# Layer 2's transposed input, written and read with a step of four floats, in a four-layer graph network kernel

## The chip, the cores and the metric

The kernel runs on one core of a Trainium2 chip, in one launch. The metric is the device time of one execution in microseconds (us), lower is better; every time shown is from the chip. The engines of a core, as the profile names them: PE is TensorE's products, PEld its weight loads (a product has a *stationary* operand, which is loaded first, and a *moving* one, which streams past it), DVE is VectorE, ACT is ScalarE, POOL is GpSimd, SP is SyncE, which here issues transfers. SBUF is the memory on the core that all engines work in, PSUM the one that TensorE writes its results to; both have 128 partitions.

## The reference

Thirty-two inputs of 512 nodes with 128 features pass through four graph layers that share one 0/1 adjacency matrix. After each layer its input is added and each node is normalised over its features. Cut to what matters:

```
x = layernorm(x + L0(x))      # attention over neighbours
x = layernorm(x + L1(x))      # attention over neighbours, elu
x = layernorm(x + L2(x))      # below
x = layernorm(x + L3(x))      # adj @ x + x, weights, each row divided by its norm

def L2(input, adj, W, e, bias):
    h0 = einsum('bnf,fg->bng', input, W[0])
    h1 = einsum('bnf,fg->bng', input, W[1])
    A = softmax(where(adj > 0, vals, NEG), axis=1)
    M = eye(N)
    return einsum('ij,bjg->big', A * M, h0) + einsum('ij,bjg->big', A * (1 - M), h1) + bias
```

All arrays are float32: `x` is (32, 512, 128), `adj` (512, 512), `W` (2, 128, 128). Layer 2 weighs a node by `W[0]` and its neighbours by `W[1]`. With the `e` of these inputs, which is all ones, every row of `A` is 1/degree over the row's neighbours, and the kernel computes layer 2 as (input W0 + (neighbour sum of input) W1) / degree.

## The kernel before

A node matrix of one input is a tile of 128 partitions by 512 columns: four *chunks* of 128 nodes, each 128 nodes by 128 features, side by side (`NCH` is 4, `P` is 128). TensorE contracts over partitions, so a product "nodes by features times weights" needs its left operand with the features on partitions. Where a layer needs its input that way, there is a transposed tile `xt`, features by 512 nodes.

The work of one input is cut into some 90 *units*, small functions that each issue one or a few instructions: `pt2` is layer 2's transposes, `xt2` the copy of their result, `py2` the neighbour sum, and so on. A unit is registered with the names of the tiles that it uses. The table `PLAN` gives each unit and input a place in one global order of some 3,260 places, or -1 if it isn't used for that input. Once, while the program is built, the order is sorted and the units are issued one after the other; each engine then works through its own instructions in that order, and semaphores make it wait for what others produce. Units of several inputs are interleaved, so that all engines have work. A unit that is registered and has no row in `PLAN` issues nothing. Buffers come from stocks of fixed size (`kind`), are taken when a tile is first used, and are given back after its last use.

Layer 2, for each of the 32 inputs:

- `pt2` (lines 170 to 174): TensorE transposes the four chunks of `x2`, with the identity as moving operand and the chunk as stationary one, into a PSUM bank `pt2` of 512 columns; chunk c goes to columns c*128 to c*128+127. For `pt0` (four inputs) and `pt1` (five inputs) the same line writes each chunk through `swapped`, as four runs of 32 columns that lie 128 apart. All other inputs get their transposed tiles of layers 0 and 1 another way: for layer 0 a reordered load and VectorE, for layer 1 VectorE's transpose (`tr1`), a transfer to DRAM (`tw1`) and four transfers back (`tb1`), which SP issues.
- `xt2` (line 178): ScalarE copies the whole bank to SBUF.
- `py2` and `y2` (lines 303 and 307): the neighbour sums, features by nodes, and their copy.
- `po2` (lines 317 and 318): for each chunk of nodes, the chunk of `y2` as stationary operand with `W[1]`, and onto it the chunk of `xt2` as stationary operand with `W[0]`. These are layer 2's last products.
- `o2s`, `v2p`, then the normalisation: the division by the degree on ScalarE (line 397), the addition of input and bias on GpSimd (line 401), statistics on VectorE (lines 360 and 362), and so on to layer 3.

Other lines that come up: 230 transposes a single column that is broadcast to 128 (the stationary operand reads one address 128 times), 217 is the product of the attention, 515 the sixteen transposes at the start that warm TensorE up, 591 transposes in bf16.

Of the kernel before, what the change touches and what calls it, by code (L numbers as in the profile page):

```python
# [10 lines left out]
F32 = mybir.dt.float32  # L11
# [7 lines left out]
P = 128  # L19
Q = 32  # L20
# [6 lines left out]
def kernel(  # L27
# [18 lines left out]
    nc = tc.nc  # L46
    B, N, F = x.shape
    NCH = N // P
# [9 lines left out]
    dram = fast.enter_context(tc.tile_pool(name="dram", bufs=1, space=bass.MemoryType.DRAM))  # L58

    def chunks(t):  # L60
        return t.rearrange("p (c f) -> p c f", c=NCH)
# [40 lines left out]
    w20, w21, w3_s = (const.tile([F, F], F32, name=n) for n in ("w20", "w21", "w3_s"))  # L102
# [12 lines left out]
    def kind(name, count, names, make):  # L115
        STOCK[name] = (count, make)
        for n in names.split():
            KIND[n] = name

    def plain(shape, dtype=F32):  # L120
        return lambda name: store.tile(list(shape), dtype, name=name)
# [13 lines left out]
    kind("rn", 12, "rn0 rn1 rn2 rn3", plain([P, 2, NCH]))  # L135
    kind("rs", 12, "rs0a rs0b rs1a rs1b", plain([P, 2]))
    kind("ss", 6, "ss", plain([P, NCH]))
    kind("dt", 4, "dt1", lambda name: dram.tile([P, N], F32, name=name))
    kind("rb", 4, "rb0 rb1", plain([P, N]))
    kind("rt", 4, "rt0 rt1", plain([P, Q]))  # L140
    kind("rd", 4, "rd0 rd1", lambda name: dram.tile([N], F32, name=name))
# [1 line left out]
    def unit(name, *tiles):  # L143
        def register(fn):
            UNITS[name] = (fn, tiles)
        return register

    def swapped(t):
        return t.rearrange("p (a c i) -> p c a i", a=NCH, c=NCH)

    def pair(t, half):
        return t[:, 2 * half : 2 * half + 2]

    @unit("ld", "x0")
    def _(b, x0):
        nc.sync.dma_start(chunks(x0), x[b].rearrange("(c p) f -> p c f", p=P))
# [7 lines left out]
    @unit("tr0", "sw0", "xt0")  # L164
    def _(b, sw, xt):
        nc.vector.transpose(swapped(xt), sw)

    for k in range(3):

        @unit(f"pt{k}", f"x{k}", f"pt{k}")  # L170
        def _(b, xk, p, k=k):
            for c in range(NCH):
                dst = swapped(p)[:, c] if k < 2 else p[:, c * P : (c + 1) * P]
                nc.tensor.transpose(dst, xk[:, c * P : (c + 1) * P], ident)  # L174

        @unit(f"xt{k}", f"pt{k}", f"xt{k}")
        def _(b, p, xt):
            nc.scalar.copy(xt, p)

    @unit("tr1", "x1", "tr1")  # L180
    def _(b, x1, tr):
        nc.vector.transpose(tr.rearrange("p (f c i) -> p c f i", f=NCH, c=NCH), x1)

    @unit("tw1", "tr1", "dt1")
    def _(b, tr, dt):
        nc.sync.dma_start(dt, tr)

    @unit("tb1", "dt1", "xt1")
    def _(b, dt, xt):
        for f in range(4):  # L190
            src = bass.AP(tensor=dt.tensor, offset=dt.offset + f * P, ap=[[N, Q], [Q * N, P // Q], [1, P]])
            nc.sync.dma_start(xt[f * Q : (f + 1) * Q, :].rearrange("p (a n) -> p a n", n=P), src)

    for k in range(2):
        for half, s in enumerate("ab"):
# [31 lines left out]
        @unit(f"pr{k}", f"pr{k}")  # L227
        def _(b, p, k=k):
            for c in range(NCH):
                nc.tensor.transpose(swapped(p)[:, c], exps[:, 2 * b + k, 0, c : c + 1].to_broadcast([P, P]), ident)  # L230
# [82 lines left out]
    @unit("po2", "y2", "xt2", "po2")  # L313
    def _(b, y, xt, p):
        for c in range(NCH):
            cols = slice(c * P, (c + 1) * P)
            nc.tensor.matmul(p[:, cols], y[:, cols], w21, start=True, stop=False)  # L317
            nc.tensor.matmul(p[:, cols], xt[:, cols], w20, start=False, stop=True)  # L318

    @unit("po3", "y3", "po3")  # L320
    def _(b, y, p):
# [89 lines left out]
    for c in range(NCH):  # L411
        cols = slice(c * P, (c + 1) * P)
# [224 lines left out]
    def _(b, p):  # L637
# [336 lines left out]
    order = sorted([(t, -1, name) for name, t in STARTS.items()]  # L974
                   + [(t, b, name) for name, ts in PLAN.items() for b, t in enumerate(ts) if t >= 0])
    users = Counter((b, t) for _, b, name in order for t in UNITS[name][1])
    home = {}
    for name, (count, make) in STOCK.items():
        FREE[name] = deque(make(f"{name}_{i}") for i in range(count))

    with tc.manual_schedule():
        first()
        for _, b, name in order:
            fn, tiles = UNITS[name]
            for t in tiles:
                if (b, t) not in home:
                    home[b, t] = FREE[KIND[t]].popleft()
            fn(b, *[home[b, t] for t in tiles])
            for t in tiles:
                users[b, t] -= 1  # L990
                if not users[b, t]:
                    FREE[KIND[t]].append(home.pop((b, t)))
# [317 lines left out]
```

## Time and profile before

| | |
|---|---|
| time, median of 3 runs | 554.61 us (552.77 to 554.64) |
| the profiled execution | 553.77 us |
| its span, first to last instruction | 552.1 us |
| mean granted TensorE clock | 0.992 |
| PE busy | 530.7 us, 96%, 4116 instructions |
| PEld busy | 501.5 us, 91%, 4116 |
| DVE busy | 499.1 us, 90%, 1913 |
| ACT busy | 472.1 us, 86%, 1868 |
| POOL busy | 405.7 us, 73%, 673 |
| line 318, products of `xt2` with `W[0]` | 256 records, 49.5 us busy, 275 ns mean |
| line 317, products of `y2` with `W[1]` | 256 records, 49.5 us busy, 275 ns mean |
| line 174, transposes from `x1` and `x2` | 148 records, 21.7 us busy, 273 ns mean |
| line 178, copies of the transposed tiles | 41 instructions, 591 ns median |

Durations on PE overlap: a product is shown from its start until its result is written, while the next has begun. Busy time of a group is the time in which at least one of its instructions runs. A product of two float32 operands shows up as two pairs of a weight load and a product, so the 128 calls of line 318 (32 inputs by 4 chunks) are 256 records; a transpose is one pair. Weight loads run beside products.

### The profile page before, as it was taken

To read this page: it belongs to the slowest core of one execution; us is meant where nothing else is said; L and a number is where in the kernel's file an instruction comes from. 1 tells how busy PE (TensorE), PEld (TensorE's weight loads), DVE (VectorE), ACT (ScalarE), POOL (GpSimd) and SP (SyncE) were. 2 spreads that over 40 slices of the span, in tenths; PEclk is the share of its full clock that TensorE was granted. 3 is DMA by queue.
4 is the path that set the end of the run, shared out by engine and by line. 5 is a ranking of instruction groups with operands and counts; after the bars stand their busy time and mean duration, and the time that the engine had idled before them with its cause. 6 is when DMAs were issued, how large, how long until landed. Compare 5 with 4: busy or idle time off the path is not lost.

```text
span 552.1 us, 13985 instructions
## 1 busy us (share of the span) xinstructions
PE 530.7 (96%) x4116; PEld 501.5 (91%) x4116; DVE 499.1 (90%) x1913; ACT 472.1 (86%) x1868; POOL 405.7 (73%) x673
## 2 busy tenths in 40 slices
PE   7999999999999999999999999999999999999971
PEld 7899999999999999999999999999999999998850
DVE  2799999999999999999999999999999986787475
ACT  3768678988898789888989898898899899989994
POOL 4223795677948868688698776778688878889973
PEclk9999999999999999999999999999999999999996
DMA  7333344536357454446453544545203211000013
GB/s 211 67 83 92 78 117 111 123 93 174 97 136 173 103 139 87 131 112 161 115 136 97 150 106 128 156 99 121 90 20 117 78 39 40 20 21 2 21 57 100
DMA packets 124449, 55.22 MB, mean 100 GB/s; under 512 B 65744, under 2 KB 113488, under 8 KB 124368
## 3 DMA queue, kind: packets, MB, share of 16 engines
q1 hardware_dynamic: 123792, 53.94, 38.4%
q8 instruction: 34, 0.56, 0.4%
q10 hardware_dynamic: 576, 0.33, 0.3%
q14 instruction: 47, 0.39, 0.2%
HBM read 38.67 MB, written 15.58 MB: 98 GB/s over the span
## 4 chain that ended last, share of the span: by engine, by line
PE 76%; DVE 11%; ACT 8%; POOL 2%; issue 1%; DMA 1%; ACTq 0%; DVEq 0%
PE ps L217 37%; PE ps L303 15%; PE ps L200 9%; DVE al L255 4%; PE ps L317 4%; PE ps L318 4%; PE ps L324 4%; PE ps L174 2%; DVE st L360 2%; ACT sq L334 1%; ACT sq L383 1%; DMA acols<-in_L_gnn_a_dst_dram 1%; ACT sq L307 1%; PE ps L230 1%; ACT sq L397 1%
## 5 line engine op out<-in xcount | busy, mean ns | idle before, releaser
L217 PE MATMUL ps<-hp,al 128*128 128x129 f32 x2048 | 244.7, 275 | 0.7 <-POOL off L579 0.5
L217 PEld LDWEIGHTS ps<-hp,al 128*128 128x128 f32 x2048 | 237.4, 191 | 2.7 <-POOL off L579 0.7
L255 DVE SCALAR_TENSOR_TENSOR al<-rb,exps,mp 128x512 f32<-128x512 f32 x216 | 145.6, 735 | 1.2 <-DMA rb<-rd 1.2
L360 DVE BATCH_NORM_STATS2 st<-sq 128x6 f32<-128x128 f32 x508 | 108.2, 274 | 11.1 <-POOL sq L401 7.7
L390 POOL TENSOR_SCALAR sq<-sq,rn 128x128 f32<-128x128 f32 x252 | 113.0, 465 | 3.5
L383 ACT ACTIVATE sq<-sq,rn 128x128 f32<-128x128 f32 x256 | 106.2, 503 | 5.8 <-POOL rn L378 5.6
L210 ACT ACTIVATE hp<-ps,exps 128x128 f32<-128x128 f32 x256 | 89.6, 431 | 0.3
L296 POOL TENSOR_TENSOR xr<-sq,xr 128x512 fp32r<-128x512 f32 x64 | 83.2, 1304 | 7.3 <-DVE st L360 3.8
L200 PE MATMUL ps<-we,sq 128*128 128x131 f32 x512 | 71.2, 277 | 0.1
L303 PE MATMUL ps<-off,xr 128*128 128x512 f32 x256 | 67.6, 406 | 0.0
L303 PE MATMUL ps<-a3t,xr 128*128 128x512 f32 x256 | 67.3, 404 | 0.2 <-POOL xr L296 0.2
L200 PEld LDWEIGHTS ps<-we,sq 128*128 128x128 f32 x512 | 65.4, 192 | 2.0 <-issue 0.5
L286 POOL TENSOR_TENSOR sq<-sq,x 128x512 f32<-128x512 f32 x32 | 41.8, 1307 | 24.0 <-DVE sq L272 13.4
L378 POOL TENSOR_TENSOR rn<-mv,rn 128x4 f32<-128x4 f32 x127 | 28.4, 229 | 41.6 <-ACT rn L374 25.3
L286 POOL TENSOR_TENSOR sq<-sq,sq 128x512 f32<-128x512 f32 x32 | 43.4, 1356 | 17.8 <-DVE sq L280 12.4
L303 PEld LDWEIGHTS ps<-a3t,xr 128*128 128x128 f32 x256 | 46.3, 189 | 10.1 <-POOL xr L296 0.6
L303 PEld LDWEIGHTS ps<-off,xr 128*128 128x128 f32 x256 | 45.9, 189 | 9.1 <-DVE sq L262 0.2
L317 PE MATMUL ps<-w,sq 128*128 128x128 f32 x256 | 49.5, 275 | 0.0
L318 PE MATMUL ps<-w,sq 128*128 128x128 f32 x256 | 49.5, 275 | 0.0
L362 DVE BATCH_NORM_AGGREGATE mv<-st 128x2 f32<-128x9 f32 x508 | 48.7, 157 | 0.0
L401 POOL TENSOR_TENSOR sq<-sq,sq 128x512 f32<-128x512 f32 x32 | 41.1, 1286 | 9.8 <-ACT sq L397 6.9
L268 ACT ACTIVATE sq<-ps,rs 128x128 f32<-128x128 f32 x128 | 39.7, 376 | 8.4 <-DVE rs L221 8.3
(116 smaller groups left out, 918.4 us busy)
## 6 DMA issues: line engine op xcount, KB each, us to landing
rb<-rd SPq DMA_DIRECT2D x54, 256.0 KB, 3.8
x<-in_x_dram SPq DMA_DIRECT2D x32, 256.0 KB, 4.0
out_dram<-sq SPq DMA_DIRECT2D x31, 256.0 KB, 2.3
sw<-in_x_dram SPq DMA_DIRECT2D x112, 64.0 KB, 3.6
dt<-sq SPq DMA_DIRECT2D x27, 256.0 KB, 2.4
sq<-dt SPq DMA_DIRECT2D x108, 64.0 KB, 2.2
rd<-rt SPq DMA_DIRECT2D x54, 2.0 KB, 1.7
an<-in_adj_dram SPq DMA_DIRECT2D x3, 256.0 KB, 4.9
```

The lines of the kernel that those rows point to most:

```text
L200: nc.tensor.matmul(twos(p)[:, c, :FE], xt[:, (2 * half + c) * P : (2 * half + c + 1) * P], ATT[k], start=True, stop=True)
L210: nc.scalar.activation(h[:, 2 * half + c, :F], twos(p)[:, c, :F], AF.Identity, bias=pc if k else 0.0, scale=pc)
L217: nc.tensor.matmul(twos(p)[:, c, : F + 1], al[:, j, rows], h[:, j, :], start=(j == 0), stop=(j == NCH - 1))
L255: nc.vector.scalar_tensor_tensor(al[:, j, :], r, exps[:, 2 * b + k, 2, j : j + 1], mask[:, j, :], op0=ALU.max, op1=ALU.mult)
L286: nc.gpsimd.tensor_add(o, o, xk)
L296: nc.gpsimd.tensor_sub(xl, xk, xh.bitcast(F32))
L303: nc.tensor.matmul(p, part[:, j * P : (j + 1) * P], mat[:, j, :], start=(i + j == 0), stop=(i + j == NCH))
L317: nc.tensor.matmul(p[:, cols], y[:, cols], w21, start=True, stop=False)
L318: nc.tensor.matmul(p[:, cols], xt[:, cols], w20, start=False, stop=True)
L360: nc.vector.bn_stats(st[:, c, :6], o[:, c * P : (c + 1) * P])
L383: nc.scalar.activation(xo[:, c * P : (c + 1) * P], o[:, c * P : (c + 1) * P], AF.Identity, bias=rn[:, 1, c : c + 1], scale=rn[:, 0, c : c ...
L390: nc.gpsimd.tensor_scalar(xo[:, c * P : (c + 1) * P], o[:, c * P : (c + 1) * P], rn[:, 0, c : c + 1], rn[:, 1, c : c + 1], op0=ALU.mult, o ...
```

## The change

A new view `mixed` of a 512-column tile takes column n*4+c as column n of chunk c: the columns of a chunk lie four floats (16 bytes) apart, and the four chunks are interleaved. `pt2` writes its transposes through it, `xt2` copies all 512 columns as before, and `po2` reads its stationary operand through it, so that what is computed stays the same. In the same edit the three units `tr1`, `tw1`, `tb1` become a loop that registers `tr2`, `tw2`, `tb2` as well, and the DRAM tile's name `dt2` is added. `PLAN` is untouched, and it has no row for the new units.

```diff
-    kind("dt", 4, "dt1", lambda name: dram.tile([P, N], F32, name=name))
+    kind("dt", 4, "dt1 dt2", lambda name: dram.tile([P, N], F32, name=name))
...
+
+    def mixed(t):
+        return t.rearrange("p (n c) -> p c n", c=NCH)
...
         @unit(f"pt{k}", f"x{k}", f"pt{k}")
         def _(b, xk, p, k=k):
             for c in range(NCH):
-                dst = swapped(p)[:, c] if k < 2 else p[:, c * P : (c + 1) * P]
+                dst = swapped(p)[:, c] if k < 2 else mixed(p)[:, c]
                 nc.tensor.transpose(dst, xk[:, c * P : (c + 1) * P], ident)
...
-    @unit("tr1", "x1", "tr1")
-    def _(b, x1, tr):
-        nc.vector.transpose(tr.rearrange("p (f c i) -> p c f i", f=NCH, c=NCH), x1)
...
+    for k in (1, 2):
+
+        @unit(f"tr{k}", f"x{k}", f"tr{k}")
+        def _(b, xk, tr, k=k):
+            nc.vector.transpose(tr.rearrange("p (f c i) -> p c f i", f=NCH, c=NCH), xk)
...
@@ -315,7 +320,7 @@
         for c in range(NCH):
             cols = slice(c * P, (c + 1) * P)
             nc.tensor.matmul(p[:, cols], y[:, cols], w21, start=True, stop=False)
-            nc.tensor.matmul(p[:, cols], xt[:, cols], w20, start=False, stop=True)
+            nc.tensor.matmul(p[:, cols], mixed(xt)[:, c], w20, start=False, stop=True)
```

More of the change, by code (lines that the diff above doesn't have):

```diff
@@ L178, in _ @@
             nc.scalar.copy(xt, p)
-    @unit("tr1", "x1", "tr1")
-    def _(b, x1, tr):
-        nc.vector.transpose(tr.rearrange("p (f c i) -> p c f i", f=NCH, c=NCH), x1)
[L184 to L192, printed above, removed]
+    for k in (1, 2):
+        @unit(f"tr{k}", f"x{k}", f"tr{k}")
+        def _(b, xk, tr, k=k):
+            nc.vector.transpose(tr.rearrange("p (f c i) -> p c f i", f=NCH, c=NCH), xk)
+        @unit(f"tw{k}", f"tr{k}", f"dt{k}")
+        def _(b, tr, dt):
+            nc.sync.dma_start(dt, tr)
+        @unit(f"tb{k}", f"dt{k}", f"xt{k}")
+        def _(b, dt, xt):
+            for f in range(4):
+                src = bass.AP(tensor=dt.tensor, offset=dt.offset + f * P, ap=[[N, Q], [Q * N, P // Q], [1, P]])
+                nc.sync.dma_start(xt[f * Q : (f + 1) * Q, :].rearrange("p (a n) -> p a n", n=P), src)
     for k in range(2):
```

## The prediction

> **What bounds the kernel now.** I read the busy table by stretches first, to see which engine is full where.
>
> ```profile
> core 0: us, PE busy (x) PEld busy (x) DVE busy (x) ACT busy (x) POOL busy (x), PEclk, DMA share, GB/s
> ...
> 72.00:200.00 128.00, 127.69 (x1013) 121.70 (x1013) 126.19 (x468) 112.70 (x432) 96.70 (x148) 1.00 0.51 125
> 200.00:350.00 150.00, 150.00 (x1192) 143.40 (x1191) 149.34 (x577) 135.26 (x549) 117.20 (x196) 1.00 0.50 126
> 350.00:480.00 130.00, 130.00 (x1011) 123.26 (x1009) 118.44 (x462) 116.90 (x471) 104.24 (x167) 1.00 0.28 76
> 480.00:524.40 44.40, 44.30 (x299) 39.92 (x298) 30.22 (x141) 41.27 (x167) 41.62 (x62) 1.00 0.04 13
> 524.40:552.10 27.70, 11.39 (x60) 8.25 (x58) 17.15 (x83) 19.55 (x100) 15.73 (x33) 0.84 0.26 78
> ```
>
> Each entry is busy us and, in brackets, instructions. From 72 to 524.4 us, where every product of `po2` lies, TensorE is idle 0.31 + 0 + 0 + 0.10 = 0.41 us. VectorE is nearly as full up to 350 us, so the plan holds two engines at their limit there, but what is added to TensorE has no gap to go into. Second, the chain of waits, which says the same in one line:
>
> ```profile
> PE 76%; DVE 11%; ACT 8%; POOL 2%; issue 1%; DMA 1%; ACTq 0%; DVEq 0%
> ```
>
> Third, the two changed lines, 318 (weight load and product) and 174 (transposes), with the two groups that I use as measures:
>
> ```profile
> L318 PEld LDWEIGHTS ps<-w,sq x256: 191/192/192, 72.7 to 524.2; 128*128 128x128 f32 x128
> L318 PE MATMUL ps<-w,sq x256: 275/275/275, 72.8 to 524.3; 128*128 128x128 f32 x128
> ...
> L174 PEld LDWEIGHTS ps<-ident,sq x148: 137/141/147, 32.5 to 517.7; 128*128 128x128 f32 x148
> L174 PE MATMUL ps<-ident,sq x148: 270/273/299, 32.6 to 517.8; 128*128 128x128 f32 x148
> ...
> L230 PEld LDWEIGHTS ps<-ident,exps x40: 133/137/139, 12.7 to 480.5; 128*128 128x128 f32 x40
> ...
> L515 PE MATMUL ps<-ident x16: 418/418/473, 1.4 to 4.7; 128*128 128x128 f32 x16
> ```
>
> Durations (min/median/max, ns) of neighbours overlap, so what an instruction costs TensorE is the step from one start to the next. The timeline gives it for one `po2`:
>
> ```profile
> 256.37 0.30 PEld L318 LDWEIGHTS ps<-w,sq 128*128 128x128 f32 x2
> 256.48 0.39 PE L318 MATMUL ps<-w,sq 128*128 128x128 f32 x2
> 256.59 0.30 PEld L317 LDWEIGHTS ps<-w,sq 128*128 128x128 f32 x2
> 256.70 0.39 PE L317 MATMUL ps<-w,sq 128*128 128x128 f32 x2
> ...
> 259.90 0.60 PE L174 MATMUL ps<-ident,sq 128*128 128x128 f32 x4
> 260.34 1.96 PE L217 MATMUL ps<-hp,al 128*128 128x129 f32 x16
> ```
>
> A call in the program is two records here (x2): 256.48 to 256.70 is 0.22 us for two, so one load with its product takes a slot of **0.111 us**. Four transposes take 260.34 - 259.90 = 0.44 us, 0.110 each. A load begins as the product ahead of it begins, 0.11 us before its own product; there is one load per product, and no slot without one.
>
> **The change, part by part.** Registered but never issued: `tr2`, `tw2`, `tb2` (PLAN has no row for them) and the name `dt2`; the stock of `dt` stays 4. No instruction is added, removed or moved, no wait and no DMA. The copy `xt2` (line 178, 0.591 us) still reads 512 neighbours. Two access patterns are left.
>
> *The write of `pt2`.* Line 174 has 148 + 16 = 164 transposes: 4 in each of 4 `pt0`, 5 `pt1` and 32 `pt2`, so 128 of `pt2` now write every fourth float. The nearest row is the same line: the 36 of `pt0` and `pt1` already write four runs of 32 with gaps between, and min and max over the 148 that read `sq` (20 of `pt1` among them) are 270 and 299 ns. Nothing there speaks for a price, and nothing for a gain: low end 0. High end: a slot twice as long. The slowest steady 128-column group is line 515's warm-up, 16 starts from 1.4 to 4.7 us, 3.3 / 15 = 0.22, against 0.110: at most 0.11 x 128 = 14.1 us. I take 0, by the nearest row, and keep 14.1.
>
> *The load of `xt2` in `po2`.* Line 318 has 256 loads, each of 128 floats per partition, so far neighbours in 512 bytes, now 16 bytes apart over 2,048. No row of the trace loads with such a step. Low end: line 230's loads read one address 128 times and take 137 ns, line 174's read 128 neighbours and take 141, so pattern has cost 4 ns at most, and even the most local one starts its products no sooner; that excludes a gain of note. In proportion to the bytes spanned, (2048 - 512) / 512 x 4 = 12 ns a load would be added, 3.1 us in all if none of it is hidden. High end: the load's fetch takes twice its slot, 0.22 in place of 0.111 as in line 515, 0.109 us more. 256 x 0.109 = 27.9 us. The ends lie far apart. I take the **high end**, because of what the load rows vary with: 98 ns for the 128x128 of line 591 in bf16, 141 for a transposing load in f32, 192 for a load of a product in f32. The same 128 columns differ by 94 ns by how they are fetched, so fetching, and not a fixed time, fills a good part of line 318's slot, and line 230's repeated address is no test of separate fetches.
>
> [...]
>
> *What hides any of it.* The product ahead of a load covers 0.111 us, and that cover is in use in full, as loads already follow one another at that step. Of idle time, 0.41 us shows; gaps below the 0.16 us by which records overlap (0.275 - 0.111) don't. At 0.111 for 3,604 records and (259.90 - 257.96) / 8 = 0.24 for the 512 of line 303, TensorE's work is 400 + 123 = 523 us of its 530.7 busy, and some 4 to 5 us of the rest are slow starts before 25 us. I let 3 us be taken up. What is late next: `o2s` on ScalarE reads each `po2`, then the sum on GpSimd and layer 2's normalisation; these have slack once TensorE sets a slower beat (ScalarE 135.26 of 150, GpSimd 117.20). VectorE, at 149.34 of 150, gains idle time. After 524.4 us no changed instruction runs, and that tail shifts as a whole.
>
> **Sum.** 27.9 + 0 - 3 = 24.9 us. The profiled execution took 553.77 us, 1.7 around its span of 552.1. 553.77 + 24.9 = 578.7; the median of the three runs, 554.61, is 0.84 higher, so **579.5 us**.
>
> **Rivals.**
>
> *Both patterns pay.* 579.5 + 14.1, about 594. For: both steps leave every neighbour behind. Against: the gapped writes of `pt0` and `pt1`, at the same duration.
>
> *Nothing is slower (the other side).* The place is line 318's slot. Its load shows 192 ns but has 0.111 us of TensorE to itself, so 81 ns overlap anyway; as long as the strided fetch ends within that slot the next product starts as before, and the time is 554.6. It decides from a fetch of 0.111 us on: below, the stride is free; each ns above costs 0.256 us. For: lines 230 and 174 differ by 4 ns. Against: no idle time anywhere if the slot is passed. The 12 ns by bytes spanned would give 554.6 + 3.1 = 557.7 less what is taken up, 555 to 558.
>
> *The write alone pays.* 554.6 + 14.1 = 568.7, some 568 after small gaps. For: in `pt2` the transposes follow one another at 0.110 too. Against: as above.
>
> *Faster.* Only a load below today's could do it, and 137 against 141 ns brought none.
>
> **How the numbers follow.** Load alone 0.30 (own range 574 to 584), both 0.26, write alone 0.13, a load price between 12 and 109 ns 0.05 (560 to 572), nothing 0.17, the small price by bytes 0.06, faster 0.03. The likeliest gives 579.5. A measurement of this kernel tells 0.5% (2.8 us) from no change: slower holds 0.30 + 0.26 + 0.13 + 0.05 and half of the 0.06, 0.77; same 0.17 + 0.03 = 0.20; faster 0.03. The range runs from 553, below the case of nothing, to 594, which leaves out the upper half of both (0.13) and the 0.03.
>
> **What would show it.** In the changed profile: line 318's loads longer than 192 ns by tens, and 0.43 us for two records of line 318 in the timeline where 0.22 stand now, while line 317 keeps 0.22; line 174's four transposes still 0.44 (0.88 if the write pays); line 178 still 0.591. TensorE stays full up to the last `po2`, which starts some 25 us later, and the tail after it keeps its 27.7 us. The forecast is wrong if line 318's step stays at 0.111, if line 174 takes over 0.11 each, or if the load slows and idle time elsewhere pays for it.

## The result, and the profile after

The changed kernel takes 581.02 us (median of 4 runs, 580.16 to 582.2) beside 554.43 us (4 runs, 552.77 to 554.64): 1.05 times as long, 95% interval 1.0466 to 1.0534. The profiled execution has a span of 580.0 us where 552.1 us stood, 27.9 us more. Lines have moved down: 174, 178, 230, 303, 317, 318 and 397 of before are 177, 181, 235, 308, 322, 323 and 402 now.

First the table by stretches, with its last bound at the end of the changed products (busy us, instructions in brackets, in the columns shown above for before):

```profile
200.00:350.00 150.00, 150.00 (x1115) 143.47 (x1115) 143.40 (x539) 128.52 (x514) 113.24 (x185) 1.00 0.51 123
350.00:500.00 150.00, 150.00 (x1112) 143.74 (x1111) 131.89 (x512) 128.03 (x511) 111.69 (x180) 1.00 0.26 73
500.00:551.20 51.20, 51.20 (x305) 46.72 (x304) 30.21 (x141) 44.10 (x175) 44.38 (x65) 1.00 0.06 17
551.20:580.00 28.80, 12.95 (x60) 9.58 (x59) 17.29 (x83) 18.84 (x96) 14.36 (x32) 0.74 0.23 67
```

TensorE (first busy entry) is full as before, yet from 200 to 350 us it gets through 1,115 products where it did 1,192. VectorE (third) falls from 149.34 to 143.40 us there: it has more idle time. The chain of waits names TensorE for 92% of the span where it named it for 76%:

```profile
PE 92%; DMA 3%; ACT 2%; DVE 1%; SPq 0%; issue 0%; POOL 0%; DVEq 0%
```

Next the changed lines, by source line (min/median/max ns, first and last start us):

```profile
L323 PEld LDWEIGHTS ps<-w,sq x256: 309/320/332, 70.9 to 551.0; 128*128 128x128 f32 x128
L323 PE MATMUL ps<-w,sq x256: 392/396/398, 71.0 to 551.1; 128*128 128x128 f32 x128
...
L177 PEld LDWEIGHTS ps<-ident,sq x148: 138/141/264, 30.7 to 543.7; 128*128 128x128 f32 x148
L177 PE MATMUL ps<-ident,sq x148: 271/273/299, 30.9 to 543.9; 128*128 128x128 f32 x148
```

The loads of `xt2` went from 192 to 320 ns, 128 ns more for 128 columns, and the products beside them from 275 to 396. The transposes that write with the step stand at 273 ns as before. The timeline of the same `po2` as shown before gives the slots:

```profile
263.64 0.38 PE L322 MATMUL ps<-w,sq 128*128 128x128 f32 x2
263.86 0.63 PE L323 MATMUL ps<-w,sq 128*128 128x128 f32 x2
264.32 0.39 PE L322 MATMUL ps<-w,sq 128*128 128x128 f32 x2
264.54 0.63 PE L323 MATMUL ps<-w,sq 128*128 128x128 f32 x2
...
268.25 0.60 PE L177 MATMUL ps<-ident,sq 128*128 128x128 f32 x4
268.68 1.96 PE L222 MATMUL ps<-hp,al 128*128 128x129 f32 x16
```

From 263.64 to 263.86 line 322's two records take 0.22 us as before; from 263.86 to 264.32 line 323's two take 0.46, so 0.23 each in place of 0.111. The lengthening is recorded in the step behind the strided product, whose own load had started 0.11 us before it, at 263.75; the sum over the pair is what counts. Four transposes take 0.43 us. So 256 records have become 0.12 us longer, 30.7 us in all. From its first start to its last, line 323 now takes 480.1 us (71.0 to 551.1) where 451.5 stood (72.8 to 524.3): 28.6 us came through there, and some 2 us went into gaps that were there. What is left to the span's 27.9 us is a start that came 1.8 us earlier and a tail that is 1.1 us longer. Neither looks like the load's doing: with the load alone (below) the tail is 27.5 us, and the run with the write alone starts these products just as early (71.1 us, against 71.0). Who waits now, by groups of lines (the last entry is idle time, and what ended it):

```profile
L402 ACT ACTIVATE sq<-ps,rdeg 128x128 f32<-128x128 f32 x128 | 36.6, 369 | 22.2 <-PE ps L323 22.0
```

ScalarE's reading of `po2` (`o2s`) waits 22.0 us for line 323 in all. That need not be a cost of its own: ScalarE is busy for 128.52 of the 150 us from 200 to 350.

### The profile page after: what moved, and what is told of

It reads as the page before. It is cut to its first block, busy times and chain, and to the rows that moved or that the text cites. A ratio compares the mean times of both kernels' runs of the same rounds, so it can differ in the third digit from the quotient of the medians.

```text
span 580.0 us, 13988 instructions
## 1 busy us (share of the span) xinstructions
PE 559.0 (96%) x4116; PEld 531.0 (92%) x4116; DVE 505.3 (87%) x1913; ACT 475.4 (82%) x1868; POOL 405.6 (70%) x673
## 4 chain that ended last, share of the span: by engine, by line
PE 92%; DMA 3%; ACT 2%; DVE 1%; SPq 0%; issue 0%; POOL 0%; DVEq 0%
PE ps L222 39%; PE ps L308 20%; PE ps L323 10%; PE ps L205 9%; PE ps L322 5%; PE ps L329 5%; PE ps L177 3%; DMA x<-in_x_dram 2%; DMA we<-in_L_gnn_W_dram 1%; PE ps L235 1%; ACT sq L388 1%; DMA sw<-in_x_dram 0%; ACT sq L339 0%; DVE al L260 0%; SPq L165 0%; PE ps L421 0%
## 5 line engine op out<-in xcount | busy, mean ns | idle before, releaser
L323 PE MATMUL ps<-w,sq 128*128 128x128 f32 x256 | 80.3, 395 | 0.0
L323 PEld LDWEIGHTS ps<-w,sq 128*128 128x128 f32 x256 | 69.6, 320 | 0.0
L308 PE MATMUL ps<-a3t,xr 128*128 128x512 f32 x256 | 68.6, 410 | 0.2 <-POOL xr L301 0.2
L406 POOL TENSOR_TENSOR sq<-sq,sq 128x512 f32<-128x512 f32 x32 | 41.0, 1280 | 23.2 <-ACT sq L402 16.4
L402 ACT ACTIVATE sq<-ps,rdeg 128x128 f32<-128x128 f32 x128 | 36.6, 369 | 22.2 <-PE ps L323 22.0
L322 PE MATMUL ps<-w,sq 128*128 128x128 f32 x256 | 49.5, 275 | 0.0
```

The source lines that it names most:

```text
L308: nc.tensor.matmul(p, part[:, j * P : (j + 1) * P], mat[:, j, :], start=(i + j == 0), stop=(i + j == NCH))
L323: nc.tensor.matmul(p[:, cols], mixed(xt)[:, c], w20, start=False, stop=True)
```

## The experiments

Each edit is against the changed kernel, each ratio against the kernel before on the same chip, with its 95% interval. The medians of before beside them were 552.98 us for the first four below, 552.25 for the strided load beside a long product and for the moving operand with a step of two, and 553.36 for the others. Where a later kernel writes or loads neighbours, it does so by the edit of one of the first two, and the edit as shown may leave that out.

**Each half of the change alone.** First the load with its step, and the write to neighbours:

```diff
-                dst = swapped(p)[:, c] if k < 2 else mixed(p)[:, c]
+                dst = swapped(p)[:, c] if k < 2 else p[:, c * P : (c + 1) * P]
```

> The step of four floats in the load of po2 alone; pt2 writes each chunk to 128 neighbouring columns as before, so po2 multiplies interleaved columns and layer 2's own term is computed from other nodes. Theory (the load pays for all of it): as after, 580 to 582 us, the start after each strided product 230 ns instead of 112. Rival (the write pays a share): shorter than after by that share, up to 14 us for a doubled transpose.

580.93 us, 1.0503 (1.0476 to 1.0531): the time of the whole change. Then the write with its step, and the load from neighbours:

```diff
-            nc.tensor.matmul(p[:, cols], mixed(xt)[:, c], w20, start=False, stop=True)
+            nc.tensor.matmul(p[:, cols], xt[:, cols], w20, start=False, stop=True)
```

> The step of four floats in the transposes' write alone; po2 loads 128 neighbours, which now hold interleaved nodes, so layer 2's own term is computed from other nodes. Theory (the write costs nothing): 554 to 555 us, four transposes in 0.44 us. Rival (the write pays a share, or a gapped write disturbs the copy that reads the bank): 556 to 568 us.

552.31 us, 0.9991 (0.9972 to 1.001): no price that can be measured. The two lines of this kernel:

```profile
L177 PE MATMUL ps<-ident,sq x148: 270/273/299, 30.9 to 516.2; 128*128 128x128 f32 x148
...
L323 PEld LDWEIGHTS ps<-w,sq x256: 191/192/192, 71.0 to 522.5; 128*128 128x128 f32 x128
```

Transposes that write every fourth float take 273 ns, and the load of neighbours is back at 192. The load is the whole cause.

**What in the load costs.** The next three vary the step. Step two, in write and load, by interleaving two chunks in each half of the tile:

```diff
-        return t.rearrange("p (n c) -> p c n", c=NCH)
+        return t.rearrange("p (h n t) -> p h t n", h=2, t=2)
...
-                dst = swapped(p)[:, c] if k < 2 else mixed(p)[:, c]
+                dst = swapped(p)[:, c] if k < 2 else mixed(p)[:, c // 2, c % 2]
...
-            nc.tensor.matmul(p[:, cols], mixed(xt)[:, c], w20, start=False, stop=True)
+            nc.tensor.matmul(p[:, cols], mixed(xt)[:, c // 2, c % 2], w20, start=False, stop=True)
```

> Write and load with a step of two floats (8 bytes): two chunks interleaved in each half of the tile; the result is the reference's. Theory A (a load pays for each read that finds its 16 bytes touched for the first and only time; two reads fall into each 16 bytes here): no price, 554 to 555 us. Theory B (price in proportion to the bytes spanned, (1024 - 512) / (2048 - 512) = one third): 40 ns a load, 10 us, 562 to 565 us. Theory C (any step above one float pays in full): 580 to 582 us.

554.07 us, 1.0026 (1.0008 to 1.0045):

```profile
L323 PEld LDWEIGHTS ps<-w,sq x256: 196/197/198, 71.1 to 523.4; 128*128 128x128 f32 x128
```

5 ns more than with neighbours, where theory B wanted 40 and theory C 128; the small rise in time, 1.1 us between the medians, is about 256 x 5 ns = 1.3 us. Step three, load alone:

```diff
-                dst = swapped(p)[:, c] if k < 2 else mixed(p)[:, c]
+                dst = swapped(p)[:, c] if k < 2 else p[:, c * P : (c + 1) * P]
...
-            nc.tensor.matmul(p[:, cols], mixed(xt)[:, c], w20, start=False, stop=True)
+            nc.tensor.matmul(p[:, cols], xt[:, c : c + 3 * P - 2 : 3], w20, start=False, stop=True)
```

> Load alone with a step of three floats (12 bytes) out of neighbouring columns; layer 2's own term is computed from other nodes. Of four reads, two share 16 bytes and two stand alone in theirs. Theory A: half of the price of step four, some 60 ns a load, 15 us, 567 to 569 us. Theory B (bytes spanned, (1536 - 512) / 1536 = two thirds): 80 ns, 20 us, 572 to 575 us. Theory C: in full, 580 to 582 us.

565.61 us, 1.0219 (1.0196 to 1.0243). The loads and, from the timeline, the slots:

```profile
L323 PEld LDWEIGHTS ps<-w,sq x256: 251/258/263, 72.7 to 538.0; 128*128 128x128 f32 x128
```

```profile
250.32 0.51 PE L323 MATMUL ps<-w,sq 128*128 128x128 f32 x2
250.67 0.39 PE L322 MATMUL ps<-w,sq 128*128 128x128 f32 x2
```

The load is 66 ns longer than on neighbours, half of step four's 128, and two records take 0.35 us, 0.064 more each. That is theory A's half, not the two thirds of B. The time came out 1.4 us under A's band: 256 x 0.064 = 16.4 us of slots, of which 12.6 us came through between the medians; the expectation had let off nothing for gaps. Step sixteen, for two of the four loads, out of a constant tile:

```diff
-            nc.tensor.matmul(p[:, cols], mixed(xt)[:, c], w20, start=False, stop=True)
+            stat = xt[:, cols] if c < 2 else em.rearrange("p c n -> p (c n)")[:, c : c + 16 * P - 15 : 16]
+            nc.tensor.matmul(p[:, cols], stat, w20, start=False, stop=True)
```

> Two of the four loads of po2's second products take 128 columns with a step of sixteen floats (64 bytes) out of the constant mask tile em, the other two the neighbouring columns of xt2; the write is contiguous. Half of layer 2's own term is computed from the mask instead of the input. Theory A (one price for each read that stands alone in its 16 bytes, however far the next is): the price of step four for half of the loads, about 120 ns for 128 loads, 15 us less what gaps take up, 566 to 569 us. Theory B (bytes spanned, (8192 - 512) / (2048 - 512) = 5 times): 600 ns for 128 loads, over 625 us.

564.31 us, 1.0201 (1.0147 to 1.0255):

```profile
L324 PEld LDWEIGHTS ps<-w,sq x128: 191/192/192, 71.0 to 533.8; 128*128 128x128 f32 x128
...
L324 PEld LDWEIGHTS ps<-w,em x128: 292/303/313, 71.9 to 535.0; 128*128 128x128 f32 x128
```

At four times the distance a load takes 303 ns, not more than the 320 at step four. Bytes spanned, five times those of step four beyond the neighbours, don't set the price. Why it is a little less is open: the tile, its address and its 0/1 values differ too. The slots agree: two strided records take 0.43 us (260.10 to 260.53), 0.10 more each, 13 us for 128. The time rose by 11.0, and so it lies 1.7 us under theory A's band, which had reckoned with 0.12.

**Where a strided load is hidden.** The transposes have a shorter load (141 ns) in nearly the same slot (0.110 against 0.111 us). Here they load with the step of four:

```diff
-                nc.tensor.transpose(dst, xk[:, c * P : (c + 1) * P], ident)
+                src = xk[:, c * P : (c + 1) * P] if k < 2 else mixed(xk)[:, c]
+                nc.tensor.transpose(dst, src, ident)
```

> The load of pt2's transposes takes every fourth column of x2, so each transpose mixes features of the four chunks; writes and po2 are contiguous. Layer 2's own term is computed from mixed features. A transpose has one load of 141 ns in a slot of 110 ns. Theory (the load's price is per read, whatever the kind of product, and the slot has no room): the load 141 + 128 = about 270 ns, slot about 230 ns, 128 transposes x 0.12 = 15 us, 566 to 569 us. Rival (a transposing load is shorter and the difference fits into the slot partly or wholly): 554 to 562 us.

554.63 us, 1.0018 (0.9991 to 1.0045): the rival held.

```profile
L178 PEld LDWEIGHTS ps<-ident,sq x148: 138/208/213, 30.7 to 516.7; 128*128 128x128 f32 x148
```

and in the timeline:

```profile
258.24 0.63 PE L178 MATMUL ps<-ident,sq 128*128 128x128 f32 x4
258.71 1.96 PE L223 MATMUL ps<-hp,al 128*128 128x129 f32 x16
```

The load did get longer, from 141 to 208 ns, but by 67 and not by 128, and four transposes went from 0.44 to 0.47 us: about 0.01 each. The theory was wrong twice: a transposing load pays about half as much, and most of that fits into the slot. Then a strided load beside a long product, line 303 of before, with 512 moving columns:

```diff
-                    nc.tensor.matmul(p, part[:, j * P : (j + 1) * P], mat[:, j, :], start=(i + j == 0), stop=(i + j == NCH))
+                    stat = mixed(part)[:, j] if k == 2 else part[:, j * P : (j + 1) * P]
+                    nc.tensor.matmul(p, stat, mat[:, j, :], start=(i + j == 0), stop=(i + j == NCH))
```

> The stationary operand of py2 (layer 2's neighbour sum, line 303 of before, moving operand of 512 columns) is loaded with a step of four floats; pt2, po2 contiguous. The sum mixes features of the four chunks. Theory (a load's price is paid only beyond what the product ahead of it covers; here a slot is 0.235 us and a strided load needs about 0.23): 554 to 558 us, with loads of about 320 ns in the trace all the same. Rival (each strided load adds its price whatever product is beside it): 256 x 0.12 = 30 us, 580 to 584 us.

556.1 us, 1.0074 (1.0042 to 1.0106), 256 strided loads as in the changed kernel:

```profile
L309 PEld LDWEIGHTS ps<-off,xr x256: 307/309/337, 63.5 to 521.4; 128*128 128x128 f32 x128
```

and in the timeline:

```profile
271.63 1.95 PE L222 MATMUL ps<-hp,al 128*128 128x129 f32 x16
273.34 2.26 PE L309 MATMUL ps<-off,xr 128*128 128x512 f32 x8
275.44 1.06 PE L205 MATMUL ps<-we,sq 128*128 128x131 f32 x8
```

The same eight before:

```profile
274.10 2.12 PE L303 MATMUL ps<-off,xr 128*128 128x512 f32 x8
276.06 1.05 PE L200 MATMUL ps<-we,sq 128*128 128x131 f32 x8
```

Eight products take 275.44 - 273.34 = 2.10 us where they took 1.96. One strided load's price, 0.12, makes up most of the 0.14: the first load of the eight stands behind a short product, the other seven behind long ones. The first three of such an eight say the same: they take 1.08 us (from 289.26) where they took 0.95 before (from 274.10), so that 0.13 of the 0.14 has come by the third product. 32 x 0.14 = 4.5 us is near the 3.9 between the medians. A load of 309 ns is nearly free where the product ahead of it lasts long enough: what is left, 0.14 - 0.12 = 0.02 us, is for all seven behind products of 512 columns.

**Other readers.** ScalarE's copy can take the step in place of the load:

```diff
+            if k < 2:
+                nc.scalar.copy(xt, p)
+            else:
+                nc.scalar.copy(chunks(xt), mixed(p))
...
-            nc.tensor.matmul(p[:, cols], mixed(xt)[:, c], w20, start=False, stop=True)
+            nc.tensor.matmul(p[:, cols], xt[:, cols], w20, start=False, stop=True)
```

> pt2 writes with the step of four, ScalarE's copy xt2 reads PSUM with that step and writes neighbours, po2 loads neighbours; the result is the reference's. Theory (the load is the only price): TensorE as before; the copy of 0.59 us may take longer, but ScalarE has idle time: 554 to 556 us. Rival (ScalarE pays for the step in PSUM, twice 0.59 us for 32 copies, and the wait moves there): up to 574 us.

553.15 us, 1.0005 (0.9975 to 1.0034): the interleaved PSUM bank can be kept at the old time. The copy doesn't notice:

```profile
L184 ACT COPY sq<-ps x32: 564/590/729, 62.1 to 519.9; 128x512 f32<-128x512 f32 x32
```

590 ns, where the plain copy took 591. Last, the moving operand, with steps of four and two out of a constant tile (the load and the write contiguous):

```diff
-            nc.tensor.matmul(p[:, cols], mixed(xt)[:, c], w20, start=False, stop=True)
+            nc.tensor.matmul(p[:, cols], xt[:, cols], mixed(mt[:, c, :])[:, c], start=False, stop=True)
```

```diff
-            nc.tensor.matmul(p[:, cols], mixed(xt)[:, c], w20, start=False, stop=True)
+            nc.tensor.matmul(p[:, cols], xt[:, cols], mt[:, c, : 2 * P].rearrange("p (n t) -> p t n", t=2)[:, 0], start=False, stop=True)
```

> The moving operand of po2's second products is read with a step of four floats out of the constant mask tile mt, in place of W[0]; load and write contiguous. Layer 2's own term uses mask columns in place of W[0]. Theory (the step costs on each read path of TensorE alike): the product's slot from 112 to about 230 ns, 580 to 582 us. Rival (the price belongs to the weight load alone): 554 to 555 us.

> As moving_strided, with a step of two floats: two reads fall into each 16 bytes. Theory A for the moving operand (a read pays that stands alone in its 16 bytes): 554 to 556 us, slot 112 to 118 ns as the load had with step two. Rival (the moving operand pays for any step): 579 to 582 us.

Step four took 579.18 us, 1.0477 (1.042 to 1.0535), step two 553.53 us, 1.002 (0.9994 to 1.0045). The timeline with step four:

```profile
252.16 0.40 PE L322 MATMUL ps<-w,sq 128*128 128x128 f32 x2
252.40 0.62 PE L323 MATMUL ps<-mt,sq 128*128 128x128 f32 x2
252.84 0.40 PE L322 MATMUL ps<-w,sq 128*128 128x128 f32 x2
```

A chunk takes 252.84 - 252.16 = 0.68 us, as with the strided load (264.32 - 263.64 = 0.68): the moving operand pays about the same price. At step two, out of the same tile, it is nearly free of it, so the tile is not the cause; its products stand at 278 ns, against 275 with `W[0]`:

```profile
L323 PE MATMUL ps<-mt,sq x256: 273/278/281, 72.9 to 524.7; 128*128 128x128 f32 x128
```

## Why the prediction was right

*The bound.* TensorE had hardly a gap to give: of the 30.7 us added to it, 28.6 came through between the first and the last changed product. For the 3 us that were let off for gaps, some 2 were measured.

*The load.* The forecast took the high end of its bounds, 0.109 us a load from the slow transposes of the start; the runs show 0.12. The term of 27.9 us was 2.8 us too small, and the 578.7 us worked out for the profiled execution stand against 581.75 measured. That the size came out so near was luck: the transposes of the start load neighbours (both their operands are the identity), so their 0.22 us has another cause, and no row of the trace tied it to a step. Nor does a row show that they warm TensorE up, as their unit's name `warm` has it: the granted clock reads 1.00 from 0 to 25 us in the kernel before, and what makes these sixteen slow is open. The wide range, 553 to 594, held also the case of nothing and that of the write alone; the narrower one of this case, 574 to 584, was given a chance of 0.30. The reason given, that fetching fills a good part of the load's slot, is borne out for this load by its rows: 192, 197, 258 and 320 ns at steps one to four with the same 128 columns. The rows of 98 and 141 ns from which it was argued could not show that, since a longer load need not lengthen its slot: the transposing load went from 141 to 208 ns, its slot only from 0.11 to 0.12 us. The estimate by bytes spanned (12 ns) is refuted by step two (197 ns, 5 more) and step sixteen (303 ns, 111 more). That the slot has no room is shown by the changed kernel; that a slot can have room, the case of "nothing is slower", by the transposes (about 0.01 us more each) and the long products (0.02 us for seven loads).

*The write.* Taken at nothing by the nearest row, the gapped writes of `pt0` and `pt1`; the kernel with the write alone shows nothing (552.31 us against 552.98). With it fall the rivals in which both pay and in which the write alone pays. These transposes take 273 ns with a step of 16 bytes as without. Whether products that accumulate pay for such a write was not tried.

*The load's price.* Five loads agree with theory A, in which a read pays that is alone in its 16 bytes. Against neighbours, at 192 ns, two reads in each 16 bytes (step two) cost 5 ns; half of the reads alone in theirs (step three) 66; all alone 128 at step four and 111 at step sixteen. A step of four floats has the full price, and a step of two is nearly free. That the 16 bytes are the cause is an inference from this pattern of prices; no row shows what a read fetches. Two readings of the slots are left that no run here separates: about 1 ns more for each read that is alone in its 16 bytes, or, as an estimate, some 1.8 ns for each 16 bytes touched, whether read once or twice (0.23 us for 128 of them, 0.22 for as many at step sixteen, 0.175 for 96, and 0.12 for the 64 at step two, from 254.79 to 255.03 for two records). The second would also explain why step two is not wholly free.

*What would show it.* Line 323's records take 0.46 us for two against the 0.43 forecast, line 322 kept 0.22, the transposes 0.43 against 0.44. The copies of line 178, 181 now, stay at 591 ns with the write alone and 588 with both. The last changed product starts 26.8 us later (551.1 against 524.3), where 25 were forecast; the tail after it took 28.8 us in this execution, where 27.7 were forecast, and 27.5 with the load alone.

## What to carry to other kernels

Keep both operands of a float32 product at a step of one or two floats where TensorE is the bound: at two the kernel took 554.07 us (write and load) and 553.53 (moving operand), against 552.98 and 552.25, and at four the slot of a 128-column product doubled, 0.111 to 0.23 us. If data must be interleaved, let the transposes write it so, or let ScalarE's copy out of PSUM undo it: both were free here (552.31 us against 552.98, 553.15 against 553.36). In these runs a load's price counted only beyond the product that covers it: a strided load of 309 to 320 ns cost 0.12 us behind 128 columns and next to nothing behind 512 (0.02 us for seven loads).

## What was not expected

The moving operand pays for the step about as much as the stationary one does (0.68 us a chunk in both cases). And a transposing load pays half of a product's load for the same step: 67 ns against 128, from 141 and 192 ns.
